# Two blocks' own expert dispatch: scatters without a pin behind the adds, its units given out three to a step of the slot stream, its gathers between the last adds

## Chip, cores and metric

The kernel runs on one NeuronCore of a Trainium2 chip. The metric is the device time in microseconds (us) of one execution of the whole program. The core has TensorE (PE in the profile, with its weight loads as PEld), VectorE (DVE), ScalarE (ACT), GpSimd (POOL) and SyncE (SP, which issues most plain transfers). Each engine works through a queue of its own, in the order in which its instructions were laid down.

## The reference, cut to what matters

The input is x of shape (4, 256, 64, 64) in float32. Layer 0 adds to x a 3x3 windowed attention over a normalized x. Layer 1 turns the pixels into 16,384 tokens of 256 channels and adds a gated moving average over 64 tokens. The last part is a mixture of experts, and it is the one that the change touches:

```python
logits = tokens @ router_w.T
rw, re = jax.lax.top_k(softmax(logits), 2)
rw = rw / rw.sum(-1)
combine = zeros((N, 8)).at[arange(N)[:, None], re].set(rw)
out = tokens
for e in range(8):
    h = gelu(tokens @ w1[e] + b1[e], approximate=False)
    y = h @ w2[e] + b2[e]
    out = out + combine[:, e:e+1] * y
```

So each token is sent to two of eight experts, each a 256x256 layer, a gelu and another 256x256 layer, and the two weighted results are added to the token.

## The kernel before

**Blocks.** The tokens are worked through in 32 blocks of 512 (`NB = 32`). A loop over g (line 1320) interleaves, by Python generators, the attention of block g (`attend`), the end of block g-1 (`tail`, to its router logits and its finished token rows), the dispatch of block g-2 (`ranks`) and the start of block g+1 (`produce`).

**Dispatch.** `ranks` counts which row of which expert's region each token gets, casts the row numbers (line 900) and scatters the token rows to DRAM: eight indirect transfers of 128 rows per block on GpSimd's queue (line 917, two for each quarter t of the block). Blocks 0 to 29 go into `rows_in`. They are cut into 127 slots of 256 rows of one expert. The last two blocks, 30 and 31, have a dispatch of their own (`apart`): they are scattered into `rows_a` and make 23 units of 128 rows (`HALVES = 23`).

**Slots.** The generator `experts` (line 1058) is the stream of slots. In round m it fetches slot m+4 (SP, line 1081), copies the expert's matrix and transposes slot m+2 (`ptx`, line 1105), gives a yield, multiplies slot m+1 by the first matrix (`psh`, line 1117, gelu at line 1123), gives a yield, writes down the add of slot m-1, and makes the two halves of the output of slot m (`psy`, line 1136, bias and weight at lines 1140 and 1141), with a yield after each half. A round is therefore four steps, the whole stream 514. The add of a slot (line 1154) is a pair of indirect transfers on GpSimd's queue which add 128 rows each to `out` in DRAM. Two slots can hold rows of the same token, so a pair waits until the pair of the slot before has landed (`behind = adds[-U:]`). There are seven buffers for slots, so the fetch of slot m+4 waits for the landed adds of slot m-3.

**Units.** `halves` (line 1195) does the same for the 23 units: fetch (SP, line 1211), matrix copy and transposes (`ptxa`, line 1219), first product (`psha`, line 1229), second product (`psya`, line 1244), bias and weight on DVE (lines 1247, 1248), and a plain store of the 128 result rows to `sums_a` (SP, line 1249). Its round m fetches unit m, transposes m-2, does the first product of m-3 and the second of m-4, with three yields: 27 rounds, 81 pieces. The units live in four buffers of two, so the fetch of unit m waits for the stores of the pair four pairs before.

**Gathers.** When all units are stored, `together` (line 1258) gathers for blocks 30 and 31 each token's two rows from `sums_a`: sixteen indirect transfers of 128 rows on GpSimd's queue (line 1268), two at a time. After eight of them DVE adds both parts to the block's held rows (line 1279) and SP stores the block (line 688).

**Order.** The program is written down once, and a planner puts each engine's instructions in order. Of the instructions that are ready by its own estimate it takes the one that was written first. `in_turn(inst, others, own)` adds to this only that an instruction stands behind others in the order. It makes no wait on the chip. In the kernel before, the scatters of blocks 30 and 31 and the gathers stand behind the add that was written last before them (`adds[-1:]`).

**The tail.** By a table of due times (`knots`, line 1302) the loop over g has taken 452 of the 514 steps when it ends. The 62 that are left are taken by the loop at line 1341, called n = 0 to 61 here. The change rewrites this loop. Before, it also takes pieces of `apart()`, that is the 81 of the units, 8 empty ones, and 24 of the gathers, spread evenly over the 62 steps: 113/62 = 1.82 to a step. So the last unit's second product is written at n = 43, the first two gathers at n = 48 and the rest by n = 60. The adds of slots 111 to 125 are written at n = 2, 6, 10 ... 58.

Of the kernel before, what the change touches and what calls it, by code (L numbers as in the profile page):

```python
# [62 lines left out]
def hybrid_block_kernel(ctx: ExitStack, tc: tile.TileContext, ins: dict, out: bass.AP):  # L63
    nc = tc.nc
    x = ins["x"]
    B, C, FW, _ = x.shape
# [4 lines left out]
    NT = TB // P  # L71
    NBI = HW // TB
    NB = B * NBI
# [18 lines left out]
    NS = NB - 2  # L92
# [6 lines left out]
    U = 2  # L99
# [6 lines left out]
    HALVES = 2 * (NB - NS) * TB // P + E - 1  # L106
# [162 lines left out]
    for n in range(2):  # L269
        t = const.tile([P, NG, HALF], FP, tag=f"pe_{n}", name=f"pe_{n}")  # L270
# [337 lines left out]
    def paced(inst):  # L608


        if latest:
            tc.add_manual_dep(
                inst.ins, latest[-1].name,
                mybir.DependencyInfo(mybir.DependencyClass.Sync, mybir.DependencyReason.DATA),
                reason="pace of the indirect transfers",
            )
        return inst
# [69 lines left out]
    def store(g, t):  # L687
        inst = nc.sync.dma_start(
            out[g * TB : (g + 1) * TB, :].rearrange("(t p) c -> p t c", p=P), t
        ).ins  # L690
        tc.declare_no_dep(inst, group="adds", reason="sums of other blocks' rows")
        tc.add_to_no_dep_group("stores", inst)
        stored.append(inst)
# [174 lines left out]
    def ranks(g):  # L868
# [3 lines left out]
        apart = k == APART  # L872
# [22 lines left out]
        own = w2p.tile([P, 2, NT, E], FP, tag="own", name=f"own_{g}")  # L895
# [9 lines left out]
        def dispatch(inst):  # L905

            for i in range(k + 1):
                tc.declare_no_dep(
                    inst, group=f"dispatch_{i}", reason="no two tokens have one row"
                )  # L910
            tc.declare_no_dep(inst, group="fetch", reason="fetched rows are not written again")
            tc.add_to_no_dep_group(f"dispatch_{k}", inst)
            dispatched[k].append(inst)
            return inst

        def give(t, c):
            return nc.gpsimd.indirect_dma_start(  # L917
                out=(rows_a if apart else rows_in)[:, :],
                out_offset=bass.IndirectOffsetOnAxis(ap=rows[:, c, t : t + 1], axis=0),
                in_=tok[:, t, :], in_offset=None,  # L920
            )


        for t in range(NT):
            for c in range(2):
                if apart:
                    in_turn(dispatch(give(t, c).ins), adds[-1:], [])
                elif g < first_of[2]:
                    dispatch(paced(give(t, c)).ins)
                else:  # L930
                    waiting.append((k, lambda t=t, c=c: in_turn(
                        dispatch(give(t, c).ins), adds[-1:], given_rows
                    )))
            yield
# [87 lines left out]
        if apart:  # L1022
            for n in range(NS, NB):
                hot, rowf = rows_of[n]
                own = w2p.tile([P, 2, NT, E], FP, tag="own", name=f"off_{n}")
# [11 lines left out]
    adds = []  # L1037
    waiting, given_rows = [], []

    def in_turn(inst, others, own):  # L1040

        for d in others:
            tc.add_manual_dep(
                inst, d.name,
                mybir.DependencyInfo(
                    mybir.DependencyClass.NoSync, mybir.DependencyReason.SCHED_ONLY
                ),
                reason="order of the indirect transfers",
            )
        own.append(inst)  # L1050
# [144 lines left out]
    def halves():  # L1195

        def load(m, what, engines, most):
            return nc.values_load(
                table[APART][0:1, what, m : m + 1], engines=list(engines), min_val=0,
                max_val=most, skip_runtime_bounds_check_because=IN_RANGE,  # L1200
            )

        xs, w1s, xc, hs = {}, {}, {}, {}

        def fetch(m):
            at = load(m, 1, [ENG.SP], E * ROOM_A)
            if m % U == 0:
                pair = xp.tile([P, U, RW], FP, tag="x", name=f"sxa_{m}")
                for n in range(U):
                    xs[m + n] = pair[:, n]  # L1210
            nc.sync.dma_start(xs[m], rows_a[bass.ds(at, P), :])  # L1211

        def pixels(m):
            e = load(m, 0, [ENG.Activation], E - 1)
            w1s[m] = xpp.tile([P, F1 + NC], FP, tag="xp", name=f"w1a_{m}")
            nc.scalar.copy(w1s[m], w1b[:, e, :])
            pt = ps_a.tile([P, NC, P], FP, tag="a", name=f"ptxa_{m}")
            for c in range(NC):
                nc.tensor.transpose(pt[:, c, :], xs[m][:, c * P : (c + 1) * P], ident)  # L1219
            xc[m] = w2p.tile([P, NC, P], FP, tag="xc", name=f"xca_{m}")  # L1220
            nc.scalar.copy(xc[m], pt)

        def hidden(m):
            w, x_ = w1s.pop(m), xc.pop(m)
            ps = ps_a.tile([P, NC, P], FP, tag="a", name=f"psha_{m}")
            for f in range(NC):
                for ci in range(NC):
                    o = ci * C + f * P
                    nc.tensor.matmul(  # L1229
                        ps[:, f, :], w[:, o : o + P], x_[:, ci, :],  # L1230
                        start=(ci == 0), stop=(ci == NC - 1),
                    )
            hs[m] = w2p.tile([P, NC, P], FP, tag="q", name=f"ha_{m}")
            for f in range(NC):
                nc.scalar.activation(
                    hs[m][:, f, :], ps[:, f, :], AF.Gelu, bias=w[:, F1 + f : F1 + f + 1]
                )

        def output(m):
            e = load(m, 0, [ENG.PE, ENG.DVE], E - 1)  # L1240
            h, x_ = hs.pop(m), xs.pop(m)
            ps = ps_a.tile([P, C], FP, tag="a", name=f"psya_{m}")
            for f in range(NC):
                nc.tensor.matmul(  # L1244
                    ps, h[:, f, :], w2[:, e, f, :], start=(f == 0), stop=(f == NC - 1)
                )
            nc.vector.tensor_add(x_[:, 0:C], ps, b2b[:, e, :])
            nc.vector.tensor_scalar_mul(x_[:, 0:C], x_[:, 0:C], x_[:, bass.ds(e + C, 1)])
            nc.sync.dma_start(sums_a[m * P : (m + 1) * P, :], x_[:, 0:C])

        for m in range(HALVES + 4):
            for back, stage in ((0, fetch), (2, pixels), (3, hidden), (4, output)):
                if 0 <= m - back < HALVES:
                    stage(m - back)
                if back:
                    yield

    def together():

        for g in range(NS, NB):  # L1260
            parts = [
                w3p.tile([P, NT, RW], FP, tag="xl_tok", name=f"own_{g}_{c}")[:, :, 0:C]
                for c in range(2)
            ]
            for t in range(NT):
                for c in range(2):
                    in_turn(
                        nc.gpsimd.indirect_dma_start(  # L1268
                            out=parts[c][:, t, :], out_offset=None, in_=sums_a[:, :],
                            in_offset=bass.IndirectOffsetOnAxis(  # L1270
                                ap=rows_of[g][:, c, t : t + 1], axis=0
                            ),
                        ).ins,
                        adds[-1:], [],
                    )
                for _ in range(3):
                    yield
            for part in parts:
                nc.vector.tensor_add(held[g], held[g], part)
            store(g, held[g])  # L1280

    def apart():
        yield from halves()
        for _ in range(REST):
            yield
        yield from together()

    REST = 8
    PIECES = 3 * (HALVES + 4) + REST + 3 * (NB - NS) * NT

    for g in range(2):
        load_xp(g)
# [11 lines left out]
    stream, done = experts(), 0  # L1304

    def follow(at):

        nonlocal done
        due = 0
        for (a, m), (b, n) in zip(knots, knots[1:]):  # L1310
            if at >= a:
                due = m + (n - m) * min(1.0, (at - a) / (b - a))
        while done < 2 * U * due:
            done += 1
            next(stream, None)
# [4 lines left out]
    for g in range(NB + 2):  # L1320
# [10 lines left out]
        n = 0  # L1331
        while gens:
            for gen in list(gens):
# [2 lines left out]
                    continue  # L1336
                n += 1
                follow(g + min(n / STEPS.get(g, 27), 0.999))
    others, given_out = apart(), 0
    left = 2 * (first_slot[-1] + 3) + U * first_slot[-1] - done  # L1340
    for n in range(left):
        next(stream, None)
        while given_out * left < (n + 1) * PIECES:
            given_out += 1
            next(others, None)
    for _ in stream:
        pass
    for _ in others:
        pass


# [56 lines left out]
```

## Time and profile before

| what | value |
|---|---|
| median of 3 runs | 1346.51 us (1344.17 to 1349.65) |
| the profiled execution's own time | 1354.12 us |
| its span in the profile | 1352.3 us |
| TensorE busy | 1183.4 us (88%) |
| VectorE, ScalarE, GpSimd busy | 931.6, 837.9, 694.5 us |
| adds, line 1154 | 254 transfers, 1592 ns of GpSimd each |
| scatters into `rows_in`, line 917 | 240 transfers, 992 ns each |
| scatters into `rows_a`, line 917 | 16 transfers |
| gathers, line 1268 | 16 transfers, 984 ns each in the median |

Times inside the profile are counted in us from the start of the span. What GpSimd shows as busy for an indirect transfer is the time in which it writes the transfer's list of rows. The data land later, and that end is seen in what waits for it. The profiled execution is 7.6 us slower than the median of the runs.

### The profile page before, as it was taken

The numbers are of one execution on the slowest core, as the hardware profiler recorded it, in microseconds if no ns is written. First come the engines' busy times: TensorE is split into PE (matmuls) and PEld (weight loads), VectorE is DVE, ScalarE is ACT, GpSimd is POOL, SyncE is SP. The second block draws the span as 40 slices with busy tenths as digits, with TensorE's granted clock in tenths as the row PEclk, the third lists the DMA queues.
The fourth block names the chain that finished last, engine by engine and source line by source line (L and its number), as shares of the span: only waits on it lengthen the run. The fifth ranks groups of instructions, "written<-read, shape, count | busy, mean of one in ns | idle before, by whom it ended". The sixth has DMA issues, their size and how long they took to land. (4 is left out here: it accounts for less than half of the span.)

```text
span 1352.3 us, 28702 instructions
## 1 busy us (share of the span) xinstructions
PE 1183.4 (88%) x8782; PEld 824.8 (61%) x8782; DVE 931.6 (69%) x4650; ACT 837.9 (62%) x1687; POOL 694.5 (51%) x618
## 2 busy tenths in 40 slices
PE   5976579899999999999989998999999998759981
PEld 4443346566666666666656666666666766648970
DVE  4477677777877878877787766777776678643332
ACT  1444357566867767777868665767776676535630
POOL 2013223545655664656655654655557566664356
PEclk9988889999999999999999998999999999988995
DMA  9764555566767767776757665666666657566644
GB/s 331 220 224 150 132 169 136 149 169 161 180 173 144 185 155 187 196 167 164 185 142 136 144 162 143 166 135 156 161 160 113 142 114 186 108 141 142 154 84 101
DMA packets 142934, 215.27 MB, mean 159 GB/s; under 512 B 16464, under 2 KB 112448, under 8 KB 138560
## 3 DMA queue, kind: packets, MB, share of 16 engines
q1 hardware_dynamic: 90656, 141.05, 33.7%
q0 software_dynamic: 49632, 71.07, 29.6%
q8 instruction: 72, 1.18, 0.4%
q10 hardware_dynamic: 2496, 1.32, 0.3%
q14 instruction: 78, 0.64, 0.2%
HBM read 120.63 MB, written 92.76 MB: 158 GB/s over the span
## 5 line engine op out<-in xcount | busy, mean ns | idle before, releaser
L1154 POOL DMA_INDIRECT out<-sx x254 | 404.3, 1592 | 394.3 <-DVE sx L1141 109.6
L1136 PE MATMUL psy<-w,h 128*128 x1016 | 280.5, 398 | 56.0 <-DVE sx L1140 33.1
L917 POOL DMA_INDIRECT rows_in<-tok,rows x240 | 238.1, 992 | 143.9 <-issue 71.0
L1136 PEld LDWEIGHTS psy<-w,h 128*128 128x128 f32 x1016 | 183.3, 193 | 147.1 <-DVE sx L1140 53.3
L1117 PE MATMUL psh<-xc,w1s 128*128 128x256 f32 x1016 | 249.0, 386 | 3.1 <-ACT h L1123 2.3
L1117 PEld LDWEIGHTS psh<-xc,w1s 128*128 128x128 f32 x1016 | 185.9, 191 | 43.3 <-issue 17.2
L1140 DVE TENSOR_TENSOR sx<-psy,b2b 128x256 f32<-128x256 f32 x254 | 107.0, 422 | 122.2 <-PE psy L1136 88.4
L1123 ACT ACTIVATE h<-psh,w1s 128x256 f32<-128x256 f32 x254 | 106.5, 470 | 53.3 <-PE psh L1117 38.2
L674 PE MATMUL pso<-mixT,vo 128*128 128x512 f32 x256 | 132.8, 642 | 0.0
L1109 ACT COPY xc<-ptx 128x512 f32<-128x512 f32 x127 | 73.6, 580 | 89.5 <-PE ptx L1105 82.7
L529 PE MATMUL psq<-x,qks 128*128 128x512 f32 x256 | 126.0, 612 | 0.5 <-ACT q L534 0.5
L1141 DVE TENSOR_SCALAR sx<-sx 128x256 f32<-128x256 f32 x254 | 90.4, 356 | 4.7 <-DVE sx L1140 0.9
L1105 PE MATMUL ptx<-ident,sx 128*128 128x128 f32 x508 | 79.5, 277 | 4.8 <-DMA sx<-rows_in 3.3
L1098 ACT COPY w1s<-w1b 128x514 f32 x127 | 79.0, 625 | 2.6 <-ACT wl L760 0.5
L1105 PEld LDWEIGHTS ptx<-ident,sx 128*128 128x128 f32 x508 | 63.9, 147 | 26.2 <-issue 16.9
L813 ACT ACTIVATE x<-x,scale 128x256 f32<-128x256 f32 x128 | 66.4, 590 | 16.6 <-DVE scale L809 10.5
L719 PE MATMUL psp<-wpr,x1c 128*128 128x136 f32 x512 | 72.7, 285 | 2.7 <-DVE y L728 1.4
L773 PE MATMUL psw<-wx,band 128*64 128x512 f32 x128 | 74.0, 678 | 0.0
L770 PE MATMUL psw<-wl,bandl 128*64 128x512 f32 x128 | 74.0, 678 | 0.0
L1123 ACT ACT_TABLE_LOAD x57 | 73.1, 1283 | 0.6
L534 ACT ACTIVATE q<-psq,qbb,irc 128x512 f32<-128x512 f32 x64 | 49.6, 776 | 37.8 <-PE psq L529 36.2
L719 PEld LDWEIGHTS psp<-wpr,x1c 128*128 128x128 f32 x512 | 66.8, 192 | 8.2 <-issue 2.5
(249 smaller groups left out, 2188.8 us busy)
## 6 DMA issues: line engine op xcount, KB each, us to landing
sx<-rows_in SPq DMA_DIRECT2D x127, 272.0 KB
xp<-in_xp SPq DMA_DIRECT2D x32, 1024.0 KB
x<-in_x SPq DMA_DIRECT2D x32, 660.0 KB
xs<-in_xs SPq DMA_DIRECT2D x32, 512.0 KB
out<-x SPq DMA_DIRECT2D x32, 512.0 KB
out<-sx POOLq DMA_INDIRECT x254
rows_in<-tok,rows POOLq DMA_INDIRECT x240
sxa<-rows_a SPq DMA_DIRECT2D x23, 136.0 KB
```

Source lines behind the costliest of these rows:

```text
L529: nc.tensor.matmul(ps.rearrange("p (r w) -> p r w", w=W), qks[:, ci, co * P : (co + 1) * P], t[:, ci, 1 : TH + 1, 1 : W + 1], start=(ci == ...
L674: nc.tensor.matmul(ps, vo[:, ci, co * P : (co + 1) * P], mixT[:, ci, :], start=(ci == 0), stop=(ci == NC - 1),)
L719: nc.tensor.matmul(ps[:, u, :], xc[:, ci, t * P : (t + 1) * P], wpr[:, ci, :], start=(ci == 0), stop=(ci == NC - 1),)
L917: return nc.gpsimd.indirect_dma_start(out=(rows_a if apart else rows_in)[:, :], out_offset=bass.IndirectOffsetOnAxis(ap=rows[:, c, t : t + ...
L1098: nc.scalar.copy(w1s, w1b[:, e, :])
L1105: nc.tensor.transpose(pt[:, c, t * P : (t + 1) * P], xs[:, t, c * P : (c + 1) * P], ident)
L1117: nc.tensor.matmul(ps[:, f, :], w1s[:, o : o + P], xc[:, ci, :], start=(ci == 0), stop=(ci == NC - 1),)
L1123: inst = nc.scalar.activation(h[:, f, :], ps[:, f, :], AF.Gelu, bias=w1s[:, F1 + f : F1 + f + 1])
L1136: nc.tensor.matmul(ps[:, t, :], h[:, f, t * P : (t + 1) * P], w2[:, e, f, :], start=(f == 0), stop=(f == NC - 1),)
L1140: nc.vector.tensor_add(ys[:, t, :], ps[:, t, :], b2b[:, e, :])
L1141: nc.vector.tensor_scalar_mul(ys[:, t, :], ys[:, t, :], xs[:, t, bass.ds(e + C, 1)])
L1154: inst = nc.gpsimd.indirect_dma_start(out=out, out_offset=bass.IndirectOffsetOnAxis(ap=xs[:, t, C + E : C + E + 1].bitcast(U32), axis=0), ...
```

## The change

Three things are altered.

- The scatters of blocks 30 and 31 are no longer put behind the last add in the order (line 927).
- The loop of the tail gives out no piece of the units in its first four steps, and then three to each step, until the 81 pieces are used up, which is at n = 30.
- The gathers come as a generator of their own. The counter `since` passes 12 at n = 35, and from then on every odd n writes two gathers: n = 35 to 49, with the adds of slots 119 to 122 written at n = 34, 38, 42 and 46. The sums of block 30 are written at n = 43, those of block 31 at n = 51. The eight empty pieces are gone.

```diff
-                    in_turn(dispatch(give(t, c).ins), adds[-1:], [])
+                    dispatch(give(t, c).ins)
...
                         adds[-1:], [],
                     )
-                for _ in range(3):
-                    yield
+                yield
             for part in parts:
                 nc.vector.tensor_add(held[g], held[g], part)
             store(g, held[g])
-
-    def apart():
-        yield from halves()
-        for _ in range(REST):
-            yield
-        yield from together()
-
-    REST = 8
-    PIECES = 3 * (HALVES + 4) + REST + 3 * (NB - NS) * NT
...
-    others, given_out = apart(), 0
+    units, own, since = halves(), together(), 0
     left = 2 * (first_slot[-1] + 3) + U * first_slot[-1] - done
     for n in range(left):
         next(stream, None)
-        while given_out * left < (n + 1) * PIECES:
-            given_out += 1
-            next(others, None)
-    for _ in stream:
-        pass
-    for _ in others:
-        pass
+        for _ in range(3 if n >= 2 * U else 0):
+            since += next(units, units) is units
+        if since > 12 and n % 2:
+            next(own, None)
+    for rest in (stream, units, own):
+        for _ in rest:
+            pass
```

## The prediction

> **What bounds the kernel now.** Only the last 150 us can change, so I read three views there: busy time by stretch of 20 us, GpSimd's timeline, and the chain of work that ended last.
>
> Busy time by stretch (columns: stretch, length, busy time and instructions of PE, PEld, DVE, ACT, POOL, then clock, DMA share, GB/s):
>
> ```profile
> 1260.00:1280.00 20.00, 20.00 (x125) 18.23 (x124) 8.10 (x21) 12.31 (x30) 7.95 (x6) 1.00 0.70 162
> 1280.00:1300.00 20.00, 20.00 (x126) 18.26 (x125) 7.68 (x20) 12.74 (x31) 7.50 (x5) 1.00 0.59 110
> 1300.00:1320.00 20.00, 14.08 (x66) 11.09 (x64) 5.71 (x15) 3.69 (x8) 12.38 (x11) 0.99 0.39 73
> 1320.00:1340.00 20.00, 4.15 (x8) 2.35 (x8) 5.04 (x10) 0.00 (x0) 15.95 (x14) 0.50 0.53 118
> 1340.00:1353.00 13.00, 0.00 (x0) 0.00 (x0) 2.45 (x2) 0.00 (x0) 4.04 (x2) 0.50 0.35 71
> ```
>
> TensorE is full at full clock while units and slots share it, and is nearly idle from 1313 on. GpSimd works to the end. GpSimd's timeline (start, duration, what, idle time before it):
>
> ```profile
> 1199.04 1.55 POOL L1154 DMA_INDIRECT out<-sx  x1 [0.30 <-issue]
> 1200.89 1.00 POOL L917 DMA_INDIRECT rows_a<-tok,rows  x1 [0.30 <-issue]
> ...
> 1209.82 0.96 POOL L917 DMA_INDIRECT rows_a<-tok,rows  x1 [0.30 <-issue]
> 1211.08 1.60 POOL L1154 DMA_INDIRECT out<-sx  x1 [0.30 <-issue]
> ...
> 1277.91 1.54 POOL L1154 DMA_INDIRECT out<-sx  x1 [3.33 <-DMA out<-sx]
> 1279.76 1.54 POOL L1154 DMA_INDIRECT out<-sx  x1 [0.30 <-issue]
> 1284.85 1.54 POOL L1154 DMA_INDIRECT out<-sx  x1 [3.54 <-DMA out<-sx]
> ...
> 1301.46 1.54 POOL L1154 DMA_INDIRECT out<-sx  x1 [5.26 <-DVE sx L1141]
> 1303.37 1.54 POOL L1154 DMA_INDIRECT out<-sx  x1 [0.37 <-DVE sxa L1248]
> 1308.27 1.01 POOL L1268 DMA_INDIRECT own<-sums_a,from  x1 [3.35 <-DMA sums_a<-sxa]
> ```
>
> Numbered back from the last pair (slot 126, at 1340.21), the pair at 1277.91 is slot 119, the one at 1301.46 slot 122, and the one at 1197.17, just above the first line, slot 109. A pair waits for the landing of the pair before. Five pairs in a row held by that alone start 7.07, 6.47, 7.04, 6.72 and 6.94 apart (1225.71 to 1232.78 to 1239.25, 1256.39 to 1263.43, 1271.19 to 1284.85), mean 6.85. With four gathers between, the landing is hidden and pairs stand 9.05 and 8.90 apart (1322.26, 1331.31, 1340.21). So there are two bounds in the tail, TensorE's queue and the chain of pairs, and the chain is what ends the program. The chain of work that ended last gives the prices on TensorE:
>
> ```profile
> 1293.53 0.22 PE ptxa L1219 x2
> 1293.74 0.89 PE psha L1229 x8
> 1294.64 0.44 PE ptx L1105 x4
> 1295.07 0.87 PE psya L1244 x4
> 1295.94 1.73 PE psh L1117 x8
> ```
>
> A unit costs 0.22 + 0.89 + 0.87 = 1.98, and a slot 0.44 + 1.73 + two output halves of 0.87 = 3.91, or 0.98 a step. That TensorE follows the written order here is seen at 1302: the last psya ends at 1302.36 (written at n = 43), and next come ptx of 125 and psh of 124, the steps n = 44 and 45. GpSimd's last pairs and gathers also stand as written: 122, two gathers, 123, six, 124, four, 125, four, 126.
>
> **The pins: 0.** Block 31's eight scatters are written between the adds of 108 and 109, and pinned behind 108. The trace has them after 109 (1197.17, 1199.04). So when the planner placed 109, their rows were not ready in its estimate, and the pin held nothing. Block 30's are pinned by quarters behind 104, 105, 105 and 106. They stand as six after 105, two after 106. Only the last two can move, ahead of 106, if that add is not ready for the planner; that would put 106 and the chain later by 0.99 + 0.31 + 0.99 + 0.30 = 2.6. The other end: if block 31's go ahead of 109, in the gap after 1193.6, the units' first fetch (1212.35) can come no earlier than SP reaches it. SP's eight blank writes end at 1204.83 and it waits on the scatters from 1206.85, so the gain is at most 5.5. I take 0, for what the order says, and keep -5.5 and +2.6.
>
> **The units ahead: +12.2.** When the last psya is written, before has taken 44 steps of the 62, after only 31. The first unit starts as before, since its data set it: in 1200 to 1216 TensorE stands 12.43 for the fetch of rows_a, and no slot work is left there that a written order could offer. From there TensorE is full in both. So the last psya ends earlier by the 13 steps not done: one output half and three slots, 0.87 + 3 x 3.91 = 12.6, at 1289.8. Call this T. But the written order has TensorE at slot 119 then, whose second output half follows T. Its pair starts at about T + 0.35 = 1290.15: the first transfer needs only the first half, the second waits for TensorE 0.87 and DVE 0.42 + 0.35, which the first transfer's 1.54 nearly covers. Before, pair 119 started at 1277.91. Between, a slot comes every 4 x 1.98 + 3.91 = 11.8, against 6.85 that the chain could do: GpSimd idles and no later stage gets this time back.
>
> **The gathers between adds: -4.1.** The first gather waits for the last store to sums_a, on GpSimd with add 120 queued behind it: before, from 1302.36 to 1308.27, 5.9. Four gathers take 5.22 (1326.09 to 1331.31). So pair 120 starts at T + 5.9 + 5.2 = T + 11.1; the landing of 119 (T + 7.2) is hidden. Then three intervals with four gathers, the mean 8.98: pair 123 at T + 38.0. Then three without, at 6.85: pair 126 at T + 58.6. From 119 to 126 that is 58.2. Before it was 1340.21 - 1277.91 = 62.3. The gathers' own 16 x 1.28 cost GpSimd the same as before. What is saved is the bunch of six and one wait. After pair 126 starts, both have the same 4.35 to 1344.56 and 7.7 to the end.
>
> The Trainium skill, DMA: Bandwidth & Descriptors, "Anatomy of one DMA — SWDGE (gpsimd) path", gives 2.0 us fixed plus bytes / 436 GB/s for a transfer. By it a 128 KB add would land 2.3 us after its issue, a pair could follow after 1.84 + 2.3 = 4.1 (an estimate from that page), the three last intervals would be 8 us shorter and the sum about +1. The trace's 3.33 and 3.54 of idle after the list is written speak against that, so the sum goes by the trace.
>
> **Units' loop: +1.** A unit now has 1.98 + 0.98 = 2.96 of TensorE time to itself, where before it was 3.59 (ptxa from 1228.81 to 1293.36, 18 units). On SP, 23 fetches and 23 stores move up past slot fetches. Unit 20's fetch waits for unit 13's store: psya of 13 starts at 1269.40, DVE ends at 1271.28, the store goes at 1272.25 and the fetch at 1276.59; a landing takes about 3.4 (1212.35 to 1215.79), so the data are there at 1280.0, 10.6 after that psya. ptxa of 20 came at 1285.52, 16.1 after it. With five rounds each 0.63 shorter it comes 13.0 after, 2.4 above the need. ScalarE per unit has 0.62 + 0.37 + 0.62, and a quarter of the slot's 0.63 + 0.58 + 0.84: 2.12 of 2.96. So the loop fits, tightly. Ends: 0, and 23 x 0.63 = 14.5 if units can go no faster than before. I take 1, near the row that fits.
>
> **DVE's sums: 0.** The sum of eight gathers (line 1279) stalls DVE, with later outputs queued behind it:
>
> ```profile
> 1322.72 1.23 DVE L1279 TENSOR_TENSOR x<-x,own 128x1024 f32<-128x1024 f32 x1 [10.59 <-DMA own<-sums_a,from]
> ```
>
> After, block 30's eighth gather is written at T + 20 and block 31's at T + 38. DVE stands until about T + 21 and T + 39, then takes 2.5. TensorE and DVE need about 4 for a slot at the half clock of 1324 to 1330, and the pairs of 122 (T + 29) and 124 (T + 45) wait for neither, if the planner puts the sums behind the outputs of 121 and 123. If not, each costs about 4: 0 to +8.
>
> **Sum.** 0 + 12.2 - 4.1 + 1 + 0 = +9.1. On the profiled execution's 1354.12 this is 1363.2. That execution is 7.6 above the median, so the median should be 1355.6.
>
> **Rivals.** *Slots keep pace (not slower).* If the planner's own estimate holds the units back (fetch and store slower than TensorE), TensorE's order goes by what is ready and slots run on at the chain's 6.85. Then pair 119 stands where it did or up to 4.3 earlier (113 at 1232.78 + 6 x 6.85 = 1273.9) and only the 4.1 of the end is gained: -4, at best -8. For: before, the order had TensorE as the shared limit only. Against: that it followed the written order step by step. It decides as soon as a unit's round takes the planner more than 2.96 of TensorE. *Scatters move up.* The first fetch is 5.5 earlier: 9.1 - 5.5 = +3.6. *Units or outputs starve.* The written order holds but the units' loop doesn't fit (+13.5 more), or DVE's sums stand ahead of 121 and 123 (+8 more): +17 to +23.
>
> **How the numbers follow.** A measurement tells about 0.5%, 6.7 us, from no change. The forecast has 0.50, with its own range +4 to +14, 0.41 of it beyond +6.7. Slots keep pace: 0.20, of it 0.11 beyond -6.7, since it can join with earlier scatters. Scatters move up: 0.10, within the bound. Starving: 0.20, all slower. So faster 0.11, same 0.09 + 0.09 + 0.10 = 0.28, slower 0.61. The range cuts about half of the first rival and the far end of the last: 1346.5 - 5.5 = 1341 to 1346.5 + 20.5 = 1367.
>
> **What would show it.** Right: block 31's scatters in one bunch behind the same pair; TensorE full from about 1225 to 1290, with adds some 12 apart in 1240 to 1290; last psya near 1290; pairs 9 apart with four gathers, then three intervals near 6.9 and an idle TensorE. Wrong: adds still 7 apart beside the units, gaps on TensorE at ptxa, or an add late in the tail released by DVE rather than by a landing.

## The result: slower by 0.55%, as forecast, and the profile after

Over nine runs each, the changed kernel takes 1350.12 us in the median and the kernel before 1343.22. The ratio is 1.0055 with a 95% interval of 1.0030 to 1.0081. Forecast were 1355.6 us and +9.1 us; measured are +6.9 us.

The spans of the two profiled executions say the opposite at first sight: 1346.4 us after, 1352.3 before. Up to the adds of the last blocks both kernels run the same instructions, and still pair 108 starts at 1190.15 in the one and at 1178.06 in the other. Executions of one program differ by that much before the tail begins. So I count everything below from the start of pair 108, the last pair ahead of anything the change could move. These lines of the kernel before give the start of pair 108, the start of pair 126 and the last second product of a unit (psya):

```profile
1190.15 1.59 POOL L1154 DMA_INDIRECT out<-sx  x1 [3.19 <-DVE row L894]
...
1340.21 1.62 POOL L1154 DMA_INDIRECT out<-sx  x1 [0.30 <-issue]
```

```profile
1301.77 0.59 PE L1244 MATMUL psya<-w,ha 128*128 x2
```

| from the start of pair 108, us | before | after |
|---|---|---|
| end of block 31's last scatter | 20.63 | 20.14 |
| first transpose of a unit | 25.64 | 25.04 |
| last second product of a unit (psya) | 112.21 | 98.48 |
| start of pair 119 | 87.76 | 100.47 |
| start of pair 126, the last | 150.06 | 157.48 |
| end of the span | 162.15 | 168.34 |

Counted so, the tail of these two executions is 6.2 us longer, which is nearly all of the 6.9 between the medians. Busy time of the changed kernel by stretch (PE, PEld, DVE, ACT, POOL, then clock, DMA share, GB/s):

```profile
1240.00:1260.00 20.00, 20.00 (x131) 18.22 (x130) 7.80 (x21) 13.71 (x35) 5.52 (x4) 1.00 0.60 152
1260.00:1280.00 20.00, 19.92 (x122) 17.86 (x121) 8.55 (x22) 11.15 (x27) 5.20 (x4) 1.00 0.50 116
1280.00:1300.00 20.00, 10.88 (x53) 9.01 (x52) 6.28 (x12) 5.88 (x12) 15.90 (x14) 0.82 0.53 99
...
1320.00:1340.00 20.00, 6.83 (x24) 5.32 (x22) 3.92 (x10) 0.84 (x2) 9.27 (x6) 0.67 0.40 49
```

TensorE is full up to 1276, when the units are through, and half empty after it. GpSimd, which ends the program, has only 5.5 and 5.2 of 20 us to do while TensorE is full: four lists of adds in each stretch. Before, it had six transfers in 1260 to 1280 and five in 1280 to 1300, 7.95 and 7.50 us. GpSimd's timeline of the changed kernel, from pair 108 on, shows what it waits for:

```profile
1178.06 1.61 POOL L1154 DMA_INDIRECT out<-sx  x1 [2.98 <-DVE comb L849]
...
1256.27 1.54 POOL L1154 DMA_INDIRECT out<-sx  x1 [7.42 <-DVE sx L1141]
1259.11 1.54 POOL L1154 DMA_INDIRECT out<-sx  x1 [1.30 <-DVE sx L1141]
1268.07 1.54 POOL L1154 DMA_INDIRECT out<-sx  x1 [7.42 <-DVE sx L1141]
1270.90 1.54 POOL L1154 DMA_INDIRECT out<-sx  x1 [1.30 <-DVE sx L1141]
1278.53 1.54 POOL L1154 DMA_INDIRECT out<-sx  x1 [6.08 <-DMA sums_a<-sxa]
...
1282.23 1.01 POOL L1268 DMA_INDIRECT own<-sums_a,from  x1 [0.31 <-issue]
...
1335.54 1.54 POOL L1154 DMA_INDIRECT out<-sx  x1 [2.90 <-issue]
```

The pairs of 117 and 118 (1256.27, 1268.07) wait 7.42 us each, and DVE's output (line 1141) releases them. The pairs that only a landing holds stand 6.5 to 7.1 us apart in the prediction's rows, so none holds these: the slots come late. They stand 11.8 us apart. The next pair, 119 (1278.53), starts 2.0 us after the end of the units' last product (the name beside it is only the event that came last; its own output ended at 1278.25). TensorE's own timeline there:

```profile
1273.79 1.89 PE L1117 MATMUL psh<-xc,w1s 128*128 128x256 f32 x8
1275.51 1.03 PE L1244 MATMUL psya<-w,ha 128*128 x4
1276.38 1.03 PE L1136 MATMUL psy<-w,h 128*128 x4
```

The scatters stand as in the kernel before, eight in one bunch behind pair 109:

```profile
1186.48 1.54 POOL L1154 DMA_INDIRECT out<-sx  x1 [0.30 <-issue]
1188.33 0.99 POOL L917 DMA_INDIRECT rows_a<-tok,rows  x1 [0.30 <-issue]
...
1198.50 1.60 POOL L1154 DMA_INDIRECT out<-sx  x1 [0.30 <-issue]
```

### The profile page after: what moved, and what is told of

It reads as the page before. It is cut to its first block, busy times and chain, and to the rows that moved or that the text cites. A ratio compares the mean times of both kernels' runs of the same rounds, so it can differ in the third digit from the quotient of the medians.

```text
span 1346.4 us, 28709 instructions
## 1 busy us (share of the span) xinstructions
PE 1178.2 (88%) x8782; PEld 821.9 (61%) x8782; DVE 930.1 (69%) x4650; ACT 838.0 (62%) x1687; POOL 695.7 (52%) x618
## 5 line engine op out<-in xcount | busy, mean ns | idle before, releaser
L674 PE MATMUL pso<-mixT,vo 128*128 128x512 f32 x256 | 128.8, 624 | 0.0
```

Source lines behind the costliest of these rows:

```text
L674: nc.tensor.matmul(ps, vo[:, ci, co * P : (co + 1) * P], mixT[:, ci, :], start=(ci == 0), stop=(ci == NC - 1),)
```

## The experiments

**Theory 1** is that of the prediction. While TensorE is full, three pieces to a step keep slots from it, so the chain of adds has nothing to add. When TensorE is through, the chain needs its 6 to 9 us for each pair that is left. **Rivals**: the gathers between the adds cost the time; the units' own loop or the uneven spread does; the chain of adds is the limit everywhere.

Each edit is shown against the changed kernel, that of block 31's scatters against the kernel before. Of longer edits only the lines that matter are shown.

The scatters' pin alone needed no run. With only line 927 changed, the planner gives all five engines the order of the kernel before, instruction for instruction. That part of the change does nothing.

### The units early, the gathers at their old steps

```diff
         for _ in range(3 if n >= 2 * U else 0):
-            since += next(units, units) is units
-        if since > 12 and n % 2:
+            next(units, None)
+        if n in (48, 50, 52, 53, 55, 57, 58, 60, 61):
+            next(own, None)
```

> The units three to a step as in the changed kernel, but the gathers written at the steps where the kernel before has them (behind the adds of 122 to 125). Theory 1, the slots fall behind because TensorE takes the units first: pair 119 still starts about 13 us late against the end of block 31's scatters, pairs 119 to 122 then stand 6.3 to 6.9 apart, 119 to 126 takes about 55 us, and the end is 1 to 2 us before that of the changed kernel, so +0.3 to +0.5% on the kernel before. Rival, the place of the gathers costs (four between each of the adds 119 to 123 hold the pairs 9 us apart): with them back at the end the loss goes, within 0.1% of the kernel before.

Measured: ratio 1.0051 (1.0018 to 1.0085). Pair 119 starts at 101.32 after pair 108 and pair 126 at 158.82, which is 57.5 between them, 2.5 us more than expected. The pairs of 119 to 122 do stand close (6.30, 8.10, 6.47), but six gathers then pile up behind one pair (12.32). So the loss comes with the units alone, and the rival of the gathers' place falls. Putting the gathers earlier was worth 2.1 us at the end (170.48 against 168.34), where I had expected it to cost 1 to 2. Between 119 and 126 it was worth only 0.5 (57.5 against 57.0).

### Two gathers to an add

```diff
+        if n in (35, 37, 39, 43, 47, 51, 55, 59, 61):
+            next(own, None)
```

> The changed kernel with its sixteen gathers laid out four behind the add of 119 and then two behind each of 120 to 125. Theory 1: pair 119 is as late as in the changed kernel (13 us), but two gathers (2.6 us) fit into the 3 us in which GpSimd waits for a landing, so from 120 on pairs stand 6.3 to 6.9 apart; 119 to 126 takes about 50 us in place of 57, and the end is 6 to 7 us before that of the changed kernel, about level with the kernel before (-0.1 to +0.1%). Rival, gathers cost their own 1.28 us each wherever they stand: 119 to 126 stays near 57 and the time at +0.5%.

GpSimd's timeline of this kernel, from pair 120 to pair 122:

```profile
1287.16 1.61 POOL L1154 DMA_INDIRECT out<-sx  x1 [0.30 <-issue]
...
1290.95 1.01 POOL L1268 DMA_INDIRECT own<-sums_a,from  x1 [0.30 <-issue]
1292.26 0.99 POOL L1268 DMA_INDIRECT own<-sums_a,from  x1 [0.30 <-issue]
1293.79 1.61 POOL L1154 DMA_INDIRECT out<-sx  x1 [0.53 <-issue]
...
1300.32 1.62 POOL L1154 DMA_INDIRECT out<-sx  x1 [0.45 <-issue]
1303.72 1.58 POOL L1154 DMA_INDIRECT out<-sx  x1 [1.79 <-DVE sx L1141]
```

Two gathers behind a pair leave 0.53 us of idle time and put the next pair 6.63 after it. They cost little there (the run without gathers, below, has 6.4); four put it 8.88 after in the changed kernel. From pair 119 (100.99) to 126 (151.55) it is 50.6, as expected, and the span ends at 163.24, 5.1 before the changed kernel and 1.1 behind the kernel before. The last line shows what is not free: the second transfer of 122 waits for an output that stands behind DVE's sum of block 30. The measured ratio is 1.0036 (1.0008 to 1.0064), which misses the expected -0.1 to +0.1% and is more than the 1.1 us of the tail make (0.08%). The interval only just reaches them, and I found nothing in the tail for the rest. The twelve times lie between 1339.58 and 1356.33, and the profiled execution, 1342.45, is one of the short ones.

### Half of the units' first product

```diff
-                for ci in range(NC):
+                for ci in range(1):
...
-                        start=(ci == 0), stop=(ci == NC - 1),
+                        start=True, stop=True,
```

> The changed kernel with half of the units' first product left out (one of two halves of the channels), which changes what the 23 units compute and takes 0.445 us of TensorE from each. Theory 1, TensorE is what the slots wait for beside the units: the units' last product comes 23 x 0.445 = 10 us earlier, pair 119 10 us earlier, the end 10 us earlier than the changed kernel's, -0.2% on the kernel before. Rival, the units' own loop of fetch, store and buffers sets the pace: TensorE gets gaps at ptxa, and the end moves by less than 3 us from the changed kernel's, still +0.4 to +0.5%.

Measured: ratio 1.0001 (0.9973 to 1.0029). The last psya comes at 90.27, pair 119 at 92.78 and the end at 160.88: 8.2, 7.7 and 7.5 us before the changed kernel. Less work of the units on TensorE pulls the slots, the pairs and the end with it, so TensorE is the limit beside the units. It is 8.2 and not 10.2 because the next limit is close: TensorE was busy 20.00 of 20 us in 1220 to 1240, but 19.61 in 1240 to 1260, with a first wait at ptxa for a unit's fetch. At about 2.5 us to a unit the units' own loop begins to show; at the change's 2.96 it does not.

### Block 31's scatters first

```diff
-                    in_turn(dispatch(give(t, c).ins), adds[-1:], [])
+                    in_turn(dispatch(give(t, c).ins), [], given_rows if g == NB - 1 else [])
```

> The kernel before with block 31's eight scatters put ahead of the add of 109 on GpSimd's queue, nothing else. Theory 1 (beside the units TensorE is the limit, so what starts it earlier ends it earlier): the scatters end about 7 us earlier, the first fetch of a unit comes when SP is through its blank writes, 5.5 us earlier, and the end comes 3 to 5.5 us earlier, -0.2 to -0.4%. Rival (the chain of the adds is the limit throughout): the pair of 109 starts 7 us later, the pair of 110 where it was, and the end does not move or comes later.

The scatters end at 13.66 after pair 108 in place of 20.63, pair 109 starts at 13.97 in place of 7.02, and pair 110 where it was (20.94). The first unit is transposed at 22.92 in place of 25.64, the last psya comes 2.6 earlier and the end 2.8 earlier (159.34). So the end follows the units' start although pair 109 is 7 us later, and the rival falls for this stretch. The gain at the end is just under the 3 to 5.5 us that I expected. The first fetch of a unit comes 20.8 us after pair 108 in place of 22.2, so 1.4 earlier and not 5.5: SP was not ready. Its timeline in this kernel:

```profile
1185.97 11.66 SPq L950 DMA_DIRECT2D rows_a<-blank  x8
1199.63 0.35 SPq L1211 DMA_DIRECT2D sxa<-rows_a  x1
```

SP takes 11.66 us to issue the eight blank writes ahead of the first fetch, more than half of it beside the scatters. Before, it took 7.40. That the scatters slow them is not shown. The last kernel below has the scatters in the same place, and there it takes 7.17 (from 1136.84 on). Even so the first fetch comes no earlier there, 20.8 us after pair 108: SP first waits up to 5.9 us for landed adds, for a slot's fetch that stands ahead. In the runs' times the 2.8 us do not stand out: the ratio is 0.9994 (0.9970 to 1.0019).

### 2.4 pieces to a step

This kernel and the two after it ran on another chip, where the kernel before takes 1292.40 us. Their ratios are to that.

```diff
+        while since < 2.4 * (n - 3):
+            since += 1
+            next(units, None)
+        if n in (43, 45, 47, 49, 51, 53, 55, 57, 59):
+            next(own, None)
```

> The changed kernel with 2.4 units' pieces to a step in place of 3, so that the last is written at n = 37 in place of 30, and the gathers four behind each of the adds of 121 to 124. Theory 1: beside the units pairs stand 3.91 + 4 x 0.8 x 1.98 = 10.2 us apart in place of 11.8; the last psya comes 7 steps x 0.98 = 6.8 us later than in the changed kernel, but two slots more are through, so the end comes 5 to 7 us earlier than the changed kernel's, measured from the start of pair 108, and level with the kernel before within 0.2%. Rival (what costs is that units begin and run apart from the even spread, or the gathers between adds): still +0.4 to +0.6%.

Measured: ratio 1.0022 (1.0006 to 1.0038). The last psya comes at 105.53, 7.1 us later than in the changed kernel, as expected. Yet the end comes 3.9 us earlier, at 164.44, where I had expected 5 to 7. So a later end of the units goes with an earlier end of the program: two more slots are through by then. With T as the end of the last psya, pair 121, the first behind it here, was held by the landing of 120 and stands at T + 3.8, where 119 stands at T + 2 in the changed kernel. Two intervals (9.96 and 7.80) are stretched. The end is still 2.3 us behind that of the kernel before, and the ratio is just past the 0.2% that I had expected at most.

### Without the gathers

```diff
-            parts = [
...
             for t in range(NT):
-                for c in range(2):
-                    in_turn(
-                        nc.gpsimd.indirect_dma_start(
...
                 yield
-            for part in parts:
-                nc.vector.tensor_add(held[g], held[g], part)
             store(g, held[g])
```

> The changed kernel without its sixteen gathers and without the sums of blocks 30 and 31, whose rows are stored without the experts' results. It shows the chain of pairs alone. Theory 1: pair 119 as late as in the changed kernel (about 100 us after pair 108), then seven intervals of 6.3 to 6.9, 45 to 48 us to pair 126 in place of 57: the four gathers in each of four gaps account for 9 to 12 us of the end, the late start for the rest. Rival (the last slots' own outputs hold the pairs): the intervals stay near 8 without gathers.

GpSimd's timeline of this kernel:

```profile
1229.19 1.55 POOL L1154 DMA_INDIRECT out<-sx  x1 [6.08 <-DMA sums_a<-sxa]
...
1235.55 1.55 POOL L1154 DMA_INDIRECT out<-sx  x1 [2.95 <-DVE sx L1141]
...
1261.53 1.55 POOL L1154 DMA_INDIRECT out<-sx  x1 [3.00 <-DMA out<-sx]
...
1267.88 1.55 POOL L1154 DMA_INDIRECT out<-sx  x1 [2.95 <-DMA out<-sx]
```

Pair 119 starts at 99.52, as late as in the changed kernel. The seven intervals to pair 126 are 6.35 to 6.57, 45.1 in all. So the chain by itself needs 6.4 us for a pair, and the rival that the last outputs hold the pairs falls. The gathers and sums add the other 12.0 of the 57.0.

### Both bounds minded

2.4 pieces to a step, block 31's scatters first, and gathers four, two, four, two, four behind the pairs of 121 to 125:

```diff
+        while since < 2.4 * (n - 3):
+            since += 1
+            next(units, None)
+        if n in (43, 45, 47, 51, 53, 55, 59, 60):
+            next(own, None)
...
-                    dispatch(give(t, c).ins)
+                    in_turn(dispatch(give(t, c).ins), [], given_rows if g == NB - 1 else [])
```

> 2.4 pieces to a step, block 31's scatters ahead of the add of 109, gathers four, two, four, two and four behind the adds of 121 to 125. If the two bounds of the tail are TensorE beside the units and the chain of pairs after them, with two gathers free in a gap and a third and fourth at 1.28 us each, pair 126 starts about 145 to 148 us after pair 108 (150 in the kernel before), and the time is -0.2 to -0.5% of the kernel before: faster than both. If sums or landings take the gain, it is level with the kernel before.

Measured: 1289.53 us, ratio 0.9974 (0.9958 to 0.9991): faster than the kernel before. The changed kernel was not timed on this chip; on the first its ratio was 1.0055. The last psya comes at 103.80 and pair 126 at 147.73, 2.3 before the kernel before, which agrees with the 2.9 us between the medians. The planner did not keep all the gathers as they were written: one slipped between the two transfers of pair 124, so that 123 and 124 have three each, and the intervals from 121 are 8.81, 6.57, 7.64, 8.18 and 8.89.

The last three rows of this table are from the second chip, and their tails are compared with that of the kernel before on the first:

| from the start of pair 108, us | last psya | pair 119 | pair 126 | end of span | ratio to before |
|---|---|---|---|---|---|
| before | 112.2 | 87.8 | 150.1 | 162.2 | 1 |
| changed | 98.5 | 100.5 | 157.5 | 168.3 | 1.0055 |
| units early, old gathers | 99.3 | 101.3 | 158.8 | 170.5 | 1.0051 |
| two gathers to an add | 99.0 | 101.0 | 151.6 | 163.2 | 1.0036 |
| half of the first product | 90.3 | 92.8 | 150.2 | 160.9 | 1.0001 |
| scatters first | 109.6 | 86.5 | 147.3 | 159.3 | 0.9994 |
| 2.4 to a step | 105.5 | 92.1 | 153.8 | 164.4 | 1.0022 |
| no gathers | 97.5 | 99.5 | 144.6 | 155.2 | one run |
| both bounds minded | 103.8 | 90.4 | 147.7 | 159.7 | 0.9974 |

## Why the prediction was right, step by step

- **The pins, 0.** Right. The planner's order is the same without them. That could be read from the trace of before: an add that was written later stood ahead of the scatters, so the pin was not what held them.
- **The units ahead, +12.2.** Right in mechanism, and two errors of size nearly cancel. Pair 119 starts 12.7 us later, counted from pair 108. The last psya comes 13.7 us earlier, where 12.6 was worked out: 0.6 of the difference is there already at the first transpose, and the planner put one more half output behind it, 0.87, which is the first psy at 1276.38 in TensorE's timeline above. So both halves of 119 follow T, the end of the last psya, and the pair starts at T + 2.0 and not at T + 0.35.
- **Units' loop, +1.** It cost next to nothing: TensorE has no gap from 1220 to the last psya. The half product's run shows that the margin was real but small.
- **Gathers between adds, -4.1.** The size is near, but its reason was wrong. From pair 119 to 126 it is 57.0 against 62.3, so -5.3. The prediction put the saving down to a bunch of six gathers and one wait. With the units early and the gathers at their old steps, still with six in a bunch, this stretch takes 57.5. So 4.8 of the 5.3 come with the early units and 0.5 with the gathers' new places. What goes is waiting: before, GpSimd idles 5.26 us ahead of pair 122 for an output, while TensorE still has units, and 3.35 us ahead of the first gather for a store (both lines are in the prediction). In the run of the units alone the interval from 121 is 6.47 in place of 9.42, and the first gather waits for nothing. By the chain alone (45.1), the kernel before takes 17.2 us more in this stretch, the units alone 12.4 and the changed kernel 12.0. Inside the sum two sizes were too large. The first interval, put at 10.75 with a wait for the last store, takes 8.80, since the first gather goes straight on (1282.23). The pairs without gathers were put at 6.85, from rows beside full transfers; in the emptier end they take 6.3, as in the run without gathers. Against these two stands the next point, which had been put at 0.
- **DVE's sums, 0 (ends 0 to +8).** Not 0. The planner laid each sum ahead of the second half of an output whose pair needed it. DVE's timeline of the changed kernel:

```profile
1287.56 0.42 DVE L1140 TENSOR_TENSOR sx<-psy,b2b 128x256 f32<-128x256 f32 x1 [0.83 <-issue]
1296.50 1.23 DVE L1278 TENSOR_TENSOR x<-x,own 128x1024 f32<-128x1024 f32 x1 [8.51 <-DMA own<-sums_a,from]
1297.64 0.35 DVE L1141 TENSOR_SCALAR sx<-sx 128x256 f32<-128x256 f32 x1
```

  The second half of 121's output was half done at 1287.98, and its weight (line 1141) came at 1297.64, after the first half of the sum. The second transfer of pair 121 starts at 1298.27. The interval from 121 is 9.89 where its neighbours with four gathers have 8.88 and 8.91, and the one from 123, without gathers, is 7.92 where the next have 6.32 and 6.29. That is 1.0 and 1.6, together +2.6 by these neighbours. Waiting for the output is the small part of it, 0.14 and 0.21 (idle times of 0.44 and 0.51 where 0.30 is usual). The large part is the list of the pair's second transfer, 2.30 both times where the neighbours have 1.54 to 1.57:

```profile
1298.27 2.30 POOL L1154 DMA_INDIRECT out<-sx  x1 [0.44 <-issue]
...
1317.14 2.30 POOL L1154 DMA_INDIRECT out<-sx  x1 [0.51 <-DVE sx L1141]
```

  Most of the rest is the landing behind 123, 3.49 where the next take 2.91 and 2.90. So the order of the sums was misjudged, but the price of about 4 that the prediction gave to such an order did not come.
- **The end.** I took the time from pair 126 to the end as equal, 4.35 and 7.7. It is 10.9 in place of 12.1, so -1.2 that the sum did not have. The list of the very last transfer takes 1.54 in place of 2.42; before, it ran beside the sum of block 31 (DVE, from 1340.53), which the early gathers moved away.
- **The sum.** 12.7 - 5.3 - 1.2 = 6.2 in the tail, against +9.1. The path and the sign were right. That the total came this near is in part luck, since the errors named above have both signs. The absolute forecast was 5.5 above the measurement. Of this, 3.3 is the kernel before itself, whose median fell from 1346.51 to 1343.22 with more runs.

Of the signs that the prediction named, the order of the scatters, adds 12 apart beside the units, pairs 9 apart with four gathers and a TensorE with gaps after the last psya are all there. Of the three last intervals near 6.9, two are 6.3 and one is 7.92. One on its list of wrong signs was there too, in a small way: transfers late in the tail released by DVE. It belongs to the point on the sums and is not another mechanism. A small slip: the rival in which slots keep pace has pair 119 up to 4.3 us earlier, and its own rows give 4.0 (1277.91 - 1273.9).

The weighing of a transfer's fixed cost can now be seen without gathers in the way. The prediction's estimate from the Trainium skill, DMA: Bandwidth & Descriptors, "Anatomy of one DMA — SWDGE (gpsimd) path", let a pair follow after about 4.1 us; the run without gathers has 6.4. The row was the better guide.

## What to carry to other kernels

When two bounds follow one another, here TensorE while units and slots share it and then a serial chain of adds, finishing one class of work early by starving the other only moves the serial part to the end. Let the work that feeds the longest serial chain go first, and fill the chain's own waits with what fits into them: two gathers in a 3 us wait were nearly free (6.5 to 6.6 us a pair against 6.4), while with four a pair took 8.8 to 8.9. And count from the last instruction that the change cannot reach: here the whole spans said 6 us shorter where the tail was 6 us longer.

## What the runs showed of the hardware

- The chip matters more than the change. The same kernel before takes 1344.96 us on one chip and 1292.40 on another, 4% apart. In the profiles nearly all of it lies ahead of the tail: pair 108 starts at 1175 to 1179 in the four runs on the first and at 1129 to 1130 in the three on the other, while the tail's own numbers agree within 2 us (last psya at 99.3 and 97.5, pair 119 at 101.3 and 99.5, for the same pace of the units). Why was not looked into.
- On the first chip, executions of one kernel lie up to 1.4% apart (1336.59 to 1354.96 for the kernel before), so a tail of a few us is better read in the trace than in the times.
- An add of 128 rows of 1 KB lands 2.9 us after its list is written when little else moves (DMA share 0.40) and 3.1 to 3.7 beside the units' transfers (share 0.59 to 0.73). The Trainium skill, DMA: Bandwidth & Descriptors, "Anatomy of one DMA — SWDGE (gpsimd) path", gives 2.0 us fixed plus the bytes at 436 GB/s, which makes 2.3 for this size (an estimate from that page). The runs have more, 1.54 + 2.90 = 4.4 counted from the start of the list, and the measurement decides.
- Behind pair 108, a list of an add takes 1.54 to 1.62 us as a rule. In the nine profiles all thirteen lists there that are longer than 2 us (2.16 to 2.53) began while a sum of eight gathers ran on DVE, and the run without gathers and sums has none above 1.60 us. Not every list beside a sum is long (1.61 at 1324.18 in the kernel before), so the cause stays open.
- SP took 7.17 to 8.43 us to issue eight plain writes of 136 KB in eight of the nine kernels, and 11.66 in one, that with block 31's scatters first. The scatters beside them are not enough to explain it, since the last kernel has them in the same place and 7.17. The cause stays open.
